# A decoder layer in fp32 on one core: normalised rows on ScalarE, the softmax factor in halves, the last products in another order, statistics at another place

## The chip, the cores and the metric

The kernel runs on one core of a Trainium2 chip. A core has engines that run side by side, each through its own list of instructions in order: TensorE (matmuls and transposes; PE in the profile, with its weight loads as PEld), VectorE (DVE), ScalarE (ACT), GpSimd (POOL), and SyncE (SP), which here issues all DMA transfers. An instruction that waits holds up everything behind it on its engine. The metric is the time of one execution on the device in microseconds (us), as the median of some runs; a profiled execution gives the trace.

## The reference

One decoder layer with three residual steps on x of shape (4, 2048, 512), fp32: a linear recurrence over the first axis (length 4), cross attention of 16 heads against 77 context rows, and a feed-forward network of hidden size 2048 whose two large matrices are followed and preceded by butterfly transforms. Each step reads a layer norm of x without gain or offset.

```python
x = x + recurrence(layernorm(x))                 # complex, diagonalised, 64 states per block of 64 features
x = x + attention(layernorm(x), ctx, Wq, Wk, Wv, Wo)   # 16 heads of 32, softmax over 77 keys
h = butterfly(layernorm(x) @ W_exp + b_exp, up_weights)
h = gelu(h + up_bias)
x = x + butterfly(h, down_weights) @ W_con + b_con + down_bias
# layernorm(x) = (x - mean) / sqrt(var + 1e-5), over the 512 features
```

## The kernel before

The 2048 columns of the second axis are cut into 16 units of 128, each with 4 rows of the first axis: a unit is a tile of 128 partitions x 4 x 512. The butterflies are multiplied into the dense matrices once, in a preparation at the start (`_prepare`, L349). The products with the dense matrices are fast-matrix-multiplication schemes: seven half-size products for queries, output projection and the up matrix (`seven`, L605; `up`, L779), and 26 products for the down matrix, in the order and with the targets of the table `DOWN` (L68). Each entry of `DOWN` names a product, a PSUM accumulator, and the parts of x that it is added to when the product is done; several products accumulate one after the other in the same accumulator, and between them its value is added to x by VectorE (L894, L896). The accumulators live in three pairs of PSUM banks, tags a, b and c (`BANK`, L73).

The work of a unit has two parts. `front` (L621) makes the three norms, the recurrence (L631), the queries (L616, ps_q), the scores (L676), the softmax (L679 to L684: minimum, exponent with sum, reciprocal of the sum, and one multiplication of all 16 heads by their factor), the transposes of the probabilities (L696) and their copies to SBUF (L699 on ScalarE, L701 on VectorE), the product with the values (L706, ps_o), the output projection (L616, ps_w) and the third norm. `feed_forward` (L753) runs eight blocks of up products with Gelu (L782 to L825), then the 26 down products (L879), then stores its rows of x (L863). While unit u is in `feed_forward`, its `step` (L765) advances `front` of unit u+1 as a generator, so that TensorE alternates between both. A tile scheduler orders each engine's list from these recordings, by its own estimates, except where `manual_schedule` (preparation, first blocks) or `keep_in_program_order` pins it.

A norm is made in three steps. `norm_stats` (L532) takes mean and variance with BN_STATS (L537) and BN_AGGR (L538) and a reciprocal root by three Newton steps on 128x4 values (L543 to L550), all on VectorE. `normed` (L553) then makes one row of 128x512 at a time with one VectorE instruction, (x - mean) * y (L563), transposes it on TensorE (L572, ps_t) and copies it with ScalarE (L573). Two row buffers (tag xn) alternate. `normed_pairs` (L576) does the same for the first norm in half rows (L590, L601, L602). After the third norm, `combine` (L742) makes the four sums of the up scheme: two on VectorE (L747, L749), two on GpSimd (L748, L750). Then the statistics of the following unit are taken (L740).

GpSimd makes the left-hand sums of the down scheme (L835), planned by `_down_plan` four products ahead. The right-hand factors of the down products lie in DRAM (dn26) and are loaded in pairs (L873) into a ring of three buffers, which the up weights of a block (L1021) share; SP issues these loads and the stores in order. The right-hand sums are made once at the hand-over from the preparation to the first unit, by GpSimd (L141) and partly VectorE (L143), and stored (L153). At the hand-over, unit 0's `front` and the preparation `prep` advance together (L981 on), where the x tile and the first statistics of unit 1 are requested at chosen steps (L984, L996).

Of the kernel before, what the change touches and what calls it, by code (L numbers as in the profile page):

```python
# [17 lines left out]
P = 128  # L18
# [52 lines left out]
        (21, "s", "+01 +11 +21"), (17, "t", "+10 +30 -01 -21"), (9, "w", "+21"), (4, "u", "+21"), (19, "z", "+10"),  # L71
        (2, "z", ""), (6, "z", "+30"), (23, "w", "+01"), (0, "u", "+31"))
# [430 lines left out]
def kernel(ctx: ExitStack, tc: tile.TileContext, x, ctx_t, ssm_vec, ssm_vt, ssm_vinv, wq_t, wk_t, wv_t,  # L503
# [49 lines left out]
    def normed(xt, res, steps):  # L553

        mv, y = norm_stats(xt)
        xnt = work.tile([P, NC, T, P], F32, tag="xnt", bufs=2, name="xnt")
        for _ in range(steps):
            yield
        rows = {}

        def row(t):
            rows[t] = work.tile([P, D], F32, tag="xn", name="xn")
            nc.vector.tensor_scalar(rows[t], xt[:, t, :], mv[:, t, 0:1], y[:, t : t + 1], ALU.subtract, ALU.mult)  # L563

        row(0)
        for t in range(T):
            if t + 1 < T:
                row(t + 1)
            yield
            ps = psum.tile([P, NC, P], F32, tag="f", name="ps_t")  # L570
            for c in range(NC):
                nc.tensor.transpose(ps[:, c, :], rows[t][:, c * P : (c + 1) * P], ident)  # L572
            nc.scalar.copy(xnt[:, :, t, :], ps)  # L573
        res.append(xnt)

    def normed_pairs(xt, res, stats):  # L576


        mv, y = stats
        xpt = work.tile([P, T // 2, D // NS, P], F32, tag="xnt", bufs=2, name="xpt")  # L580
# [4 lines left out]
        def row(n):  # L585
            i, h = divmod(n, 2)
            rows[n] = work.tile([P, NC, 2, NS], F32, tag="xn", name="xp")
            for k in range(2):
                t = 2 * i + k
                nc.vector.tensor_scalar(rows[n][:, :, k, :], xt[:, t, h * half : (h + 1) * half].rearrange("p (f n) -> p f n", n=NS),  # L590
                                        mv[:, t, 0:1], y[:, t : t + 1], ALU.subtract, ALU.mult)
# [29 lines left out]
    def front(u, xt, res, wq=None):  # L621
# [3 lines left out]
        yield from normed_pairs(xt, got, stats.pop(u) if u in stats else norm_stats(xt, tc.keep_in_program_order if u else lambda i: i))  # L625
# [11 lines left out]
        yield from normed(xt, got, 2)  # L637
# [30 lines left out]
        probs = [None] * T  # L668
        ot = work.tile([P, NC, T, P], F32, tag="xnt", bufs=2, name="ot")
        for t in range(T + 1):  # L670
            if t < T:
# [11 lines left out]
                nc.vector.reciprocal(sm, sm)  # L683
                nc.vector.tensor_tensor(pr, pr, sm.unsqueeze(2).to_broadcast([P, NH, NK]), ALU.mult)  # L684
                probs[t] = pr
                yield
            if t == 0:
                yield
                continue
            yield  # L690
            pr, tt = probs[t - 1], t - 1
            pts = work.tile([P, NC, 4, P], F32, tag="pt", bufs=1, name="pt")
            for g in range(NC):
# [4 lines left out]
                if g % 2:  # L698
                    nc.scalar.copy(pt, pt_ps[0:NK])  # L699
                else:  # L700
                    nc.vector.tensor_copy(pt, pt_ps[0:NK])  # L701
            po = psum.tile([P, NC, P], F32, tag="f", name="ps_o")
# [32 lines left out]
        yield from normed(xt, got, 4)  # L735
# [17 lines left out]
    def feed_forward(u, xt, rhs, other):  # L753
# [111 lines left out]
        for kind, where, *rest in plan:  # L865
# [31 lines left out]
            if i == 19:  # L897
                store(1)
                store(2)
            if i == 6:  # L900
                store(0, slice(0, D // 2))
                store(3, slice(0, D // 2))
            if i == 23:
                store(0, slice(D // 2, D))
# [30 lines left out]
    with ExitStack() as stack, tc.manual_schedule(engines={E.PE, E.SP, E.Pool}):  # L935
# [45 lines left out]
        for n, _ in enumerate(prep):  # L981
            if n == 27:
                _right_sums(nc, 0, wdn, rings, True)
            if n == 36:  # L984
                stats[1] = norm_stats(xts[1], tc.keep_in_program_order)
# [10 lines left out]
            if n == 24:  # L996
# [105 lines left out]
```

## Time and profile before

| | us |
|---|---|
| median of 3 runs | 2639.95 (2635.13 to 2644.54) |
| profiled execution | 2642.55 |
| its span in the trace | 2640.8 |
| one unit in the steady part (2216.1 to 2370.8) | 154.7 |
| TensorE busy in the span | 2537.6 (96%) |
| VectorE, ScalarE, GpSimd busy | 1519.4, 1071.6, 924.2 |
| mean granted TensorE clock | 0.995 of full |

In the lines of the profile a group is given by line of the kernel, engine, operation, output and inputs, with its count, its time, and the idle time before it with what ended it. In a list of waits each line has who waited for whom, the total in us, how many times, and the longest. In a timeline each line has start, duration, engine, line and operation, and in brackets the idle time just before it. A matmul in fp32 appears as two records. In the table of stretches a line has the length, the busy time and count of TensorE, its weight loads, VectorE, ScalarE and GpSimd, the granted clock, the busy share of the DMA engines and GB/s. Lines are those of the kernel before.

### The profile page before, as it was taken

How to read it: one execution, taken by the hardware profiler on the slowest of the kernel's cores; microseconds unless marked ns; L12 is line 12 of the kernel's file. 1: busy time of each engine (PE TensorE's matmuls, PEld its weight loads, DVE VectorE, ACT ScalarE, POOL GpSimd, SP SyncE). 2: the span in 40 equal slices, each digit the busy share in tenths (PEclk: the TensorE clock that was granted, in tenths of full speed). 3: DMA queues.
4: the chain of work that ended last, by engine and by line, in shares of the span. 5: the costliest groups of instructions: out<-in, count | busy, mean ns of one | idle time of the engine just before them, and what ended most of it. 6: DMA issues, size and time to landing. Idle time of an engine off the chain costs nothing.

```text
span 2640.8 us, 39542 instructions
## 1 busy us (share of the span) xinstructions
PE 2537.6 (96%) x14280; PEld 2127.7 (81%) x14280; DVE 1519.4 (58%) x3452; ACT 1071.6 (41%) x3327; POOL 924.2 (35%) x885
## 2 busy tenths in 40 slices
PE   8897999999999999999999999999999999999999
PEld 5776888787878878787887878888787878878788
DVE  6667565645646565564656556465655646465543
ACT  2452616235261523526153362624326262442621
POOL 4436422514233251422315142241514224152424
PEclk9998999999999999999999999999999999999999
DMA  5728444444545444464544446453444635344456
GB/s 177 255 80 296 162 146 161 162 154 140 209 142 168 164 153 162 136 213 136 174 144 168 154 135 215 140 181 134 164 168 136 215 132 177 144 149 168 136 185 237
DMA packets 145523, 440.70 MB, mean 167 GB/s; under 512 B 20913, under 2 KB 52785, under 8 KB 142513
## 3 DMA queue, kind: packets, MB, share of 16 engines
q1 hardware_dynamic: 145330, 438.18, 48.3%
q8 instruction: 114, 1.87, 0.3%
q14 instruction: 79, 0.65, 0.1%
HBM read 398.27 MB, written 39.86 MB: 166 GB/s over the span
## 4 chain that ended last, share of the span: by engine, by line
PE 77%; DVE 10%; ACT 8%; DMA 2%; POOL 1%; issue 1%; DVEq 0%; POOLq 0%; ACTq 0%; SPq 0%
PE ps_a L879 11%; PE ps_b L782 11%; PE ps_a L782 7%; PE ps_q L616 7%; PE ps_c L782 7%; PE ps_b L879 6%; PE ps_c L879 6%; PE ps_w L616 6%; ACT pr L681 4%; PE ps_sc L676 3%; PE ps_s L631 3%; PE ps_pt L696 3%; PE ps_o L706 2%; PE ps_t L572 2%; ACT L787 1%; ACT L681 1%
## 5 line engine op out<-in xcount | busy, mean ns | idle before, releaser
L835 POOL TENSOR_TENSOR arena<-arena 128x512 f32<-128x512 f32 x448 | 593.6, 1336 | 1457.8 <-ACT arena L787 822.3
L787 ACT ACTIVATE arena<-arena,hbias 128x256 f32<-128x256 f32 x384 | 191.7, 507 | 343.4 <-DVE arena L822 265.5
L681 ACT ACTIVATE pr<-ps_sc,low 128x77 f32<-128x77 f32 x960 | 296.6, 333 | 23.9 <-DVE low L679 22.9
L782 PE MATMUL ps_b<-arena 128*128 128x256 f32 x1128 | 293.8, 381 | 3.8 <-DVE arena L813 3.8
L573 ACT COPY xnt<-ps_t 128x512 f32<-128x512 f32 x128 | 72.0, 585 | 450.8 <-PE ps_t L572 450.8
L879 PE MATMUL ps_a<-arena 128*128 128x256 f32 x896 | 220.0, 381 | 18.8 <-DVE xt L894 12.7
L782 PEld LDWEIGHTS ps_b<-arena 128*128 128x128 f32 x1128 | 209.8, 191 | 31.3 <-DVE arena L813 4.2
L679 DVE TENSOR_REDUCE low<-ps_sc 128x4 f32<-128x308 f32 x240 | 114.7, 478 | 164.0 <-PE ps_sc L676 159.1
L681 ACT ACTIVATION_READ_ACCUMULATOR pr<-ps_sc,low 128x1 f32 x960 | 206.0, 215 | 0.0
L879 PEld LDWEIGHTS ps_a<-arena 128*128 128x128 f32 x896 | 165.5, 190 | 50.0 <-DVE xt L894 16.7
L879 PE MATMUL ps_b<-arena 128*128 128x256 f32 x768 | 201.4, 380 | 0.5 <-DVE xt L894 0.5
L782 PE MATMUL ps_a<-xnt,arena 128*128 128x256 f32 x752 | 196.3, 380 | 0.0
L676 PE MATMUL ps_sc<-kbd,qt 128*128 128x308 f32 x480 | 170.2, 442 | 0.0
L879 PE MATMUL ps_a<-w,arena 128*128 128x256 f32 x640 | 160.9, 382 | 5.9 <-ACT arena L787 5.8
L798 ACT COPY arena<-ps_a 128x256 f32<-128x256 f32 x128 | 48.2, 376 | 290.3 <-PE ps_a L782 290.3
L782 PEld LDWEIGHTS ps_a<-xnt,arena 128*128 128x128 f32 x752 | 143.3, 191 | 22.0
L696 PE MATMUL ps_pt<-ident,pr 128*77 128x128 f32 x1024 | 153.4, 279 | 4.2 <-DVE pt L701 3.9
L616 PE MATMUL ps_q<-xnt,wq 128*128 128x256 f32 x640 | 151.2, 379 | 2.2 <-POOL xnt L661 2.2
L696 PEld LDWEIGHTS ps_pt<-ident,pr 128*77 128x77 f32 x1024 | 119.2, 147 | 41.8 <-DVE pt L701 15.7
L879 PEld LDWEIGHTS ps_b<-arena 128*128 128x128 f32 x768 | 137.6, 190 | 16.0 <-DVE xt L894 0.9
L879 PEld LDWEIGHTS ps_a<-w,arena 128*128 128x128 f32 x640 | 118.8, 190 | 26.8 <-ACT arena L787 11.4
L616 PEld LDWEIGHTS ps_q<-xnt,wq 128*128 128x128 f32 x640 | 121.5, 190 | 19.0 <-POOL xnt L661 2.6
(232 smaller groups left out, 4860.9 us busy)
## 6 DMA issues: line engine op xcount, KB each, us to landing
arena<-dn SPq DMA_DIRECT2D x256, 512.0 KB, 3.9
w<-dn SPq DMA_DIRECT2D x160, 512.0 KB, 3.4
arena<-up SPq DMA_DIRECT2D x79, 896.0 KB, 4.5
wq<-wq SPq DMA_DIRECT2D x16, 1792.0 KB, 8.8
w<-up SPq DMA_DIRECT2D x32, 896.0 KB, 6.5
xt<-in_x SPq DMA_DIRECT2D x11, 1024.0 KB, 6.6
dn<-arena SPq DMA_DIRECT2D x8, 1152.0 KB, 5.8
arena<-up SPq DMA_DIRECT2D x30, 256.0 KB, 4.1
```

The lines of the kernel that those rows point to most:

```text
L572: nc.tensor.transpose(ps[:, c, :], rows[t][:, c * P : (c + 1) * P], ident)
L573: nc.scalar.copy(xnt[:, :, t, :], ps)
L616: nc.tensor.matmul(tiles[key][:, r, :], lhsT=lhs(i, r, k), rhs=rhs(i, r, k), start=key == i and r == 0 and k == 0, stop=k == 1, skip_group ...
L631: nc.tensor.matmul(ps[:, 2 * i : T, f * NS : (f + 1) * NS], lhsT=xpt[:, i, c * (P // NS) + f, :], rhs=gt[:, 0 : T - 2 * i, :], start=i == ...
L676: nc.tensor.matmul(ps[:, 0 : 4 * NK], lhsT=qt[:, g, t, :], rhs=kbd[:, t, g, :], start=True, stop=True)
L679: nc.vector.tensor_reduce(low, sc, AX.X, ALU.min)
L681: nc.scalar.activation(pr[:, 4 * g + h, :], sc[:, h, :], AF.Exp, bias=low[:, h : h + 1], scale=-1.0, accum_out=sm[:, 4 * g + h : 4 * g + h ...
L696: nc.tensor.transpose(pt_ps[0:NK, j, :], pr[:, 4 * g + j, :], ident)
L782: nc.tensor.matmul(ps, lhsT=w[:, c, :], rhs=rhs[i - 1][:, c], start=first and c == 0, stop=c == 1, skip_group_check=True)
L787: nc.scalar.activation(out, x, AF.Gelu, bias=hbias[:, b : b + 1])
L835: nc.gpsimd.tensor_tensor(place(p), place(x), place(y), ALU.add if op == "+" else ALU.subtract)
L879: nc.tensor.matmul(ps, lhsT=left[:, j, :], rhs=pair[:, n, j, :], start=first and j == 0, stop=j == NB // 4 - 1, skip_group_check=True)
```

## The change

Five things change; the arithmetic stays the same up to rounding.

- The rows of the third norm of every unit, and of all norms of unit 1, are made by ScalarE as Identity(x * y + nb) instead of VectorE. `shifts` makes nb = -mean * y with one 128x4 VectorE instruction and writes it over the means.
- The multiplication of the probabilities by their factor is split into two halves of 8 heads. For rows 1 to 3 it is recorded after the copies of the row before, and no longer before its transposes.
- The last products of `DOWN` run as 9, 19, 4, 23, 2, 6, 0 in place of 9, 4, 19, 2, 6, 23, 0.
- The stores of a unit follow product 2 (rows 1 and 2) and product 6 (row 0 whole, half of row 3), in place of products 19, 6 and 23.
- At the hand-over, the x tile of unit 1 is requested at step 15 instead of 24, and its first statistics at step 19 instead of 36.

```diff
@@ -68,8 +68,8 @@
 DOWN = ((11, "x", "+01"), (12, "y", "+30"), (5, "x", "+00"), (16, "y", "+31"), (1, "p", "+11"), (18, "q", "+20"),
         (22, "r", "+31"), (13, "o", "+00"), (25, "w", "+00"), (14, "x", "+10 +11"), (15, "y", "+21 +20"), (3, "v", "+20"),
         (20, "z", "+31"), (7, "w", "+20"), (8, "u", "-00 -10"), (10, "z", "+11"), (24, "v", "+00 +10"),
-        (21, "s", "+01 +11 +21"), (17, "t", "+10 +30 -01 -21"), (9, "w", "+21"), (4, "u", "+21"), (19, "z", "+10"),
-        (2, "z", ""), (6, "z", "+30"), (23, "w", "+01"), (0, "u", "+31"))
+        (21, "s", "+01 +11 +21"), (17, "t", "+10 +30 -01 -21"), (9, "w", "+21"), (19, "z", "+10"), (4, "u", "+21"),
+        (23, "w", "+01"), (2, "z", ""), (6, "z", "+30"), (0, "u", "+31"))
 BANK = dict(x="a", y="b", p="c", q="c", r="c", o="c", w="a", v="b", z="a", u="b", s="c", t="c")
 
 
@@ -550,9 +550,15 @@
             nc.vector.scalar_tensor_tensor(y, w, 1.5, y, ALU.add, ALU.mult)
         return mv, y
 
-    def normed(xt, res, steps):
+    def shifts(mv, y):
+
+        nc.vector.scalar_tensor_tensor(mv[:, :, 0], mv[:, :, 0], -1.0, y, ALU.mult, ALU.mult)
+        return mv[:, :, 0]
+
+    def normed(xt, res, steps, by_act):
 
         mv, y = norm_stats(xt)
+        nb = shifts(mv, y) if by_act else None
         xnt = work.tile([P, NC, T, P], F32, tag="xnt", bufs=2, name="xnt")
         for _ in range(steps):
             yield
@@ -560,6 +566,9 @@
 
         def row(t):
             rows[t] = work.tile([P, D], F32, tag="xn", name="xn")
+            if by_act:
+                nc.scalar.activation(rows[t], xt[:, t, :], AF.Identity, bias=nb[:, t : t + 1], scale=y[:, t : t + 1])
+                return
             nc.vector.tensor_scalar(rows[t], xt[:, t, :], mv[:, t, 0:1], y[:, t : t + 1], ALU.subtract, ALU.mult)
 
         row(0)
@@ -573,10 +582,11 @@
             nc.scalar.copy(xnt[:, :, t, :], ps)
         res.append(xnt)
 
-    def normed_pairs(xt, res, stats):
+    def normed_pairs(xt, res, stats, by_act):
 
 
         mv, y = stats
+        nb = shifts(mv, y) if by_act else None
         xpt = work.tile([P, T // 2, D // NS, P], F32, tag="xnt", bufs=2, name="xpt")
         half = D // 2
         yield
@@ -587,8 +597,11 @@
             rows[n] = work.tile([P, NC, 2, NS], F32, tag="xn", name="xp")
             for k in range(2):
                 t = 2 * i + k
-                nc.vector.tensor_scalar(rows[n][:, :, k, :], xt[:, t, h * half : (h + 1) * half].rearrange("p (f n) -> p f n", n=NS),
-                                        mv[:, t, 0:1], y[:, t : t + 1], ALU.subtract, ALU.mult)
+                out, x = rows[n][:, :, k, :], xt[:, t, h * half : (h + 1) * half].rearrange("p (f n) -> p f n", n=NS)
+                if by_act:
+                    nc.scalar.activation(out, x, AF.Identity, bias=nb[:, t : t + 1], scale=y[:, t : t + 1])
+                else:
+                    nc.vector.tensor_scalar(out, x, mv[:, t, 0:1], y[:, t : t + 1], ALU.subtract, ALU.mult)
 
         row(0)
         for n in range(T):
@@ -622,7 +635,7 @@
 
 
         got = []
-        yield from normed_pairs(xt, got, stats.pop(u) if u in stats else norm_stats(xt, tc.keep_in_program_order if u else lambda i: i))
+        yield from normed_pairs(xt, got, stats.pop(u) if u in stats else norm_stats(xt, tc.keep_in_program_order if u else lambda i: i), u == 1)
         xpt = got.pop()
         for c in range(NC):
             ps = psum.tile([P, T, P], F32, tag="f", name="ps_s")
@@ -634,7 +647,7 @@
             nc.vector.tensor_tensor(xc, ps, xc, ALU.add)
             yield
 
-        yield from normed(xt, got, 2)
+        yield from normed(xt, got, 2, u == 1)
         xnt = got.pop()
         qt = work.tile([P, NC, T, P], F32, tag="qt", bufs=1, name="qt")
         if wq is None:
@@ -666,6 +679,12 @@
                           4: plus(q21, q21), 3: plus(q12, q12)})
 
         probs = [None] * T
+
+        def divided(pr, sm):
+            nc.vector.reciprocal(sm, sm)
+            for h in (slice(0, NH // 2), slice(NH // 2, NH)):
+                nc.vector.tensor_tensor(pr[:, h], pr[:, h], sm[:, h].unsqueeze(2).to_broadcast([P, NH // 2, NK]), ALU.mult)
+
         ot = work.tile([P, NC, T, P], F32, tag="xnt", bufs=2, name="ot")
         for t in range(T + 1):
             if t < T:
@@ -680,15 +699,14 @@
                     for h in range(4):
                         nc.scalar.activation(pr[:, 4 * g + h, :], sc[:, h, :], AF.Exp, bias=low[:, h : h + 1], scale=-1.0,
                                              accum_out=sm[:, 4 * g + h : 4 * g + h + 1])
-                nc.vector.reciprocal(sm, sm)
-                nc.vector.tensor_tensor(pr, pr, sm.unsqueeze(2).to_broadcast([P, NH, NK]), ALU.mult)
-                probs[t] = pr
+                probs[t] = pr, sm
                 yield
             if t == 0:
+                divided(*probs[0])
                 yield
                 continue
             yield
-            pr, tt = probs[t - 1], t - 1
+            pr, tt = probs[t - 1][0], t - 1
             pts = work.tile([P, NC, 4, P], F32, tag="pt", bufs=1, name="pt")
             for g in range(NC):
                 pt_ps = psum.tile([P, 4, P], F32, tag="f", name="ps_pt")
@@ -699,6 +717,8 @@
                     nc.scalar.copy(pt, pt_ps[0:NK])
                 else:
                     nc.vector.tensor_copy(pt, pt_ps[0:NK])
+            if t < T:
+                divided(*probs[t])
             po = psum.tile([P, NC, P], F32, tag="f", name="ps_o")
             for g in range(NC):
                 for j in range(4):
@@ -732,7 +752,7 @@
         yield from seven((1, 6, 2, 7, 5, 4, 3), lambda i, r, k: left[i][:, k, r, :], lambda i, r, k: wo[:, i - 1, k, :], "w",
                          {1: spread, 6: onto(r12), 2: onto(r11), 7: onto(r22), 5: onto(r22), 4: onto(r21), 3: onto(r12)})
 
-        yield from normed(xt, got, 4)
+        yield from normed(xt, got, 4, True)
         res.append((u, xt, got.pop()))
         if u:
             combine(res[-1][2], res)
@@ -894,14 +914,12 @@
                     nc.vector.tensor_tensor(r, x, r, ALU.add)
                 else:
                     nc.vector.tensor_tensor(r, r, x, ALU.subtract)
-            if i == 19:
+            if i == 2:
                 store(1)
                 store(2)
             if i == 6:
-                store(0, slice(0, D // 2))
+                store(0)
                 store(3, slice(0, D // 2))
-            if i == 23:
-                store(0, slice(D // 2, D))
         store(3, slice(D // 2, D))
         for _ in other:
             pass
@@ -979,10 +997,10 @@
             run(prep, first)
         run(prep, prep, first, first, first, first)
         for n, _ in enumerate(prep):
+            if n == 19:
+                stats[1] = norm_stats(xts[1], tc.keep_in_program_order)
             if n == 27:
                 _right_sums(nc, 0, wdn, rings, True)
-            if n == 36:
-                stats[1] = norm_stats(xts[1], tc.keep_in_program_order)
             if n == 31:
                 _right_stores(nc, 0, wdn, rings, dn26, (2, 0))
             if n not in (24, 25):
@@ -993,7 +1011,7 @@
                 nc.gpsimd.tensor_tensor(wo[:, 6], wo[:, 2], wo[:, 6], ALU.subtract)
                 nc.gpsimd.tensor_tensor(wo[:, 5], wo[:, 2], wo[:, 4], ALU.subtract)
                 nc.gpsimd.tensor_tensor(wo[:, 3], wo[:, 1], wo[:, 5], ALU.subtract)
-            if n == 24:
+            if n == 15:
                 xts[1] = load_x(1)
             if n == 25:
                 early.append(work.tile([P, 7, 2, P], F32, tag="qt", bufs=1, name="w_second"))
```

## The prediction

> **What bounds the kernel now.** I read the busy times first, then the busy times of one steady stretch, then TensorE's waits, and then the timelines of the places where it waits.
>
> ```profile
> PE 2537.6 (96%) x14280; PEld 2127.7 (81%) x14280; DVE 1519.4 (58%) x3452; ACT 1071.6 (41%) x3327; POOL 924.2 (35%) x885
> ...
> 2216.10:2370.80 154.70, 151.00 (x850) 127.03 (x849) 89.41 (x206) 64.76 (x204) 51.05 (x44) 1.00 0.47 162
> ```
>
> TensorE is busy 2537.6 of 2640.8 us; the second line is one unit of 154.7 us with 151.0 us of TensorE at full clock. The change removes no matmul, so it can only win from the 103 us of TensorE's idle time (3.7 us in that unit). These waits make most of what I use:
>
> ```profile
> PE ps_o L706 <- DVE pt L701: 20.2, 30, 1.0
> PE ps_a L879 <- DVE xt L894: 12.7, 10, 1.3
> PE ps_t L572 <- DVE xn L563: 7.6, 5, 4.0
> ...
> PE ps_a L879 <- DVE arena L894: 6.2, 5, 1.3
> ...
> PE ps_b L782 <- DVE arena L801: 5.3, 1, 5.3
> ...
> PE ps_b L782 <- DVE arena L813: 3.8, 1, 3.8
> PE ps_c L879 <- DMA arena<-dn: 2.9, 3, 1.7
> ```
>
> Total, times and longest: the first recurs twice in each unit, the two waits on L894 are one wait once in each of 15 units (12.7 + 6.2 = 18.9 us, 1.26 each), and L563, L801 and L813 are single waits, nearly all between 195 and 250 us, where the weights' preparation hands over to the first unit.
>
> **Part 1: the last six products.** One unit's end, TensorE and then VectorE:
>
> ```profile
> 2379.31 1.89 PE L879 MATMUL ps_a<-arena 128*128 128x256 f32 x8
> 2381.03 1.46 PE L879 MATMUL ps_a<-w,arena 128*128 128x256 f32 x6
> 2383.76 3.72 PE L879 MATMUL ps_a<-arena 128*128 128x256 f32 x16 [1.27 <-DVE xt L894]
> ```
>
> ```profile
> 2380.19 1.79 DVE L747 TENSOR_TENSOR arena<-xnt 128x512 f32<-128x512 f32 x1 [0.70 <-ACT xnt L573]
> 2382.09 0.69 DVE L749 TENSOR_TENSOR arena<-xnt,arena 128x512 f32<-128x512 f32 x1
> 2382.70 0.69 DVE L537 BATCH_NORM_STATS2 st<-xt 128x6 f32<-128x512 f32 x1
> 2383.30 0.40 DVE L894 TENSOR_TENSOR xt<-ps_a,xt 128x256 f32<-128x256 f32 x1
> ```
>
> Product 19 ends near 2381.0. Its addition to x (L894) stands on VectorE behind L747, L749 and a BN_STATS, and is done at 2383.7. Product 2 accumulates into the same bank z, so it starts at 2383.76, after three matmuls of product 23 that were put ahead. In the new order 19 runs before 4, then come 23 and 2: two products of 1.73 us lie between 19 and 2. In the changed instruction order the addition of 19 also stands ahead of L747. So it is read near 2379.5 and product 2 wants the bank at 2382.8: 3.3 us of cover. Late next is the addition of 4 (bank u, behind L747, L749 and one BN_STATS, near 2383.7), which product 0 needs at 2386.2.
>
> Then TensorE enters the next unit 1.27 us earlier, while VectorE does not: L747 still starts after the last copy of L573 (2380.1). From it follow L749, the statistics of the next unit, four L590 and L801 of its first block. I put L801's end at 2391.2 where TensorE's seventh product needs it at 2391.7: 0.5 us left. I take 1.2 us for each of 15 units: 18 us, ends 0 (the wait comes back at L801) and 18.9.
>
> Its stores: SP issues five instead of six per unit, 1 MB as before. The early half store that stood ahead of the last dn loads is gone. The load of the second block's weights (896 KB) now stands behind the store of row 0, which waits for product 23's addition (near 2384.8), where before it stood behind two stores and waited for a buffer until 2387.08. That buffer now held products 23 and 2 and is free at 2384.5. Landing 5.2 us after its issue gives 2390.5; TensorE needs it near 2392.5. So it is hidden with 2 us to spare. GpSimd's sums for the new order wait at most until product 17 is done (2374.9), and the last is needed at 2386: nothing.
>
> **Part 2: the factor in halves.**
>
> ```profile
> 2473.94 1.08 PE L706 MATMUL ps_o<-pt,vsb 77*32 77x128 f32 x32 [1.01 <-DVE pt L701]
> ...
> 2471.84 1.44 DVE L684 TENSOR_TENSOR pr<-pr,sm 128x1232 f32<-128x1232 f32 x1
> 2473.20 0.68 DVE L701 COPY pt<-ps_pt 77x512 f32<-77x512 f32 x1
> ```
>
> (First line TensorE's timeline, then VectorE's.) The copy L701 that the first ps_o needs queues behind L684. With halves, about 0.7 us each, the changed order puts it between them: it ends near 2473.3, so ps_o could start 0.6 us sooner. But two instructions later TensorE needs a dn load, and that load does not move, because it is issued when a block's weights are released, before this place:
>
> ```profile
>   PEld ps_c L879: 6.7, 8
>   PE ps_c L879: 2.9, 3
> ...
> DMA to landing us min/median/max: 3.0/3.7/7.4
> ```
>
> (Who waited for the dn loads, times, and their landing.) In 8 of 15 units the weight load already waits for it; there the 0.6 us is given back at once. In the other 7 some 0.5 us stays: 3.5 us, ends 0 and 15 x 0.6 = 9. The second wait on L701 (0.38 us per unit) has ScalarE's ot copy ahead of it and stays. The second halves are needed only at the next transposes, 8 us later; 64 more instructions cost VectorE some 0.06 us each, under its 42% of idle time.
>
> **Part 3: rows on ScalarE.** Removed from VectorE: 4 rows per unit of the third norm, 738 ns each by the mean of L563, and unit 1's rows of all three norms; added: one tiny operation (0.17 us) per norm. No row of the trace is an Identity from SBUF of this shape. The nearest is Gelu with a bias, 128x256 from SBUF, 507 ns; 256 more elements cost 209 ns by the copies (585 for 128x512, 376 for 128x256): 0.72 us. [...] The order of ScalarE shows no more table loads than before.
>
> **Part 4: the hand-over, statistics sooner and unit 1's rows.**
>
> ```profile
> 202.50 2.05 PE L782 MATMUL ps_b<-arena,w_first 128*128 128x256 f32 x4 [5.29 <-DVE arena L801]
> ...
> 245.19 1.08 PE L572 MATMUL ps_t<-ident,xn 128*128 128x128 f32 x4 [3.99 <-DVE xn L563]
> ...
> 194.86 0.65 DVE L544 TENSOR_SCALAR vi<-v 128x4 int32<-128x4 int32 x1
> ```
>
> The 5.29 us go: VectorE no longer has 18 statistics instructions ahead of L801. They now stand ahead of unit 0's own third norm, 5 us of work, so its first transpose (182.34) comes 3 to 7 us later. (128x4 operations take 0.16 us when GpSimd is idle and 0.65 beside its sums, as the last line shows.) So far nothing is won. What sets the end is a chain that the change leaves: GpSimd's right-hand sums, their dn stores (6.4 us to land), then sixteen L143 on VectorE that wait for them, and behind those L813, the statistics and the rows that end at 248. With L590 (3.6 us for the first four) and L563 off VectorE, the last sums start about 1.5 us sooner and the four transposes, fed by rows of 0.72 us from ScalarE, end 1 to 3 us sooner. The x load of unit 1 is moved ahead of the first weights on SP and still waits for its tile until 159.9; the weights then land near 166, needed at 193. The w load no longer waits for L498 until 203.6, which frees 0.9 us.
>
> [...] I take 2.5 us for this part, ends -6 and +8.
>
> **Sum.** 18 + 3.5 + 0 + 2.5 = 24 us. The profiled execution took 2642.55 us (2640.8 span, 1.75 around it), so it would be 2618.5; the median of the runs shown lies 2.6 lower, at 2639.95: **2616**.
>
> **Rivals.** (A) The boundary wait returns at L801 or the xp rows because VectorE's chain from L747 isn't sooner: 0.5 us of slack speaks against it, its small size for it. Some 0.4 us kept of 1.26: 6 + 3.5 + 2.5 = 12, 2628. (B) The covers are larger than I read: 18.9 + 9 + 7 = 35, 2605; the DMA rows speak against it. (C) The reorder moves the wait to another bank, and no part does anything: 2639; the two products between speak against it. (D) Slower: at each boundary the row 0 store blocks SP ahead of the second block's weights. It decides when product 23's addition comes later than 2386.8 (2 us after my figure); each us beyond costs 15 us. To lose, it must come 3.6 us late: 2650 at 4.3 us. L747 at 1.79 us beside GpSimd is the only thing near that could stretch.
>
> **Chances.** Main case 0.63 (2609 to 2622), A 0.13, B 0.13, C 0.05, D 0.06. All but C and D are faster by over 0.3% (7.9 us, about what a measurement of this kernel can tell); a bad hand-over puts 0.01 of A within: faster 0.88, same 0.06, slower 0.06. The range leaves out C, D and half of B: 2605 to 2631.
>
> **What would show it.** Right: no wait of ps_a L879 on L894; a steady unit of about 153.2 us; waits on pt L701 near half, those on dn loads larger; the xn row on ScalarE between 0.65 and 0.85 us with no wait of ps_t in steady units; the first transpose of the hand-over later, L801's 5.3 us gone. Wrong: a new wait of ps_b L782 on L801 or of ps_a L782 on weights in every unit, or a hand-over that ends later than 250 us.

## The result and the profile after

| | before | after |
|---|---|---|
| median of 4 runs each, taken together | 2637.83 us | 2616.86 us |
| ratio, 95% interval | | 0.9919 (0.9894 to 0.9944) |
| ratio in a second set of runs | | 0.9891 (0.9871 to 0.9911) |
| span of the profiled execution | 2640.8 us | 2613.2 us |

The prediction was 2616 (2605 to 2631). The sum came out nearly right, but its terms did not: part 1 was worth more than its 18 us, part 2 about its 3.5, and part 4 nothing that these runs can tell from 0. That the sum lies so near the measured median is partly luck, as the section on the prediction says.

The page's busy times, after:

```profile
PE 2537.3 (97%) x14280; PEld 2130.7 (82%) x14280; DVE 1478.2 (57%) x3458; ACT 1126.2 (43%) x3403; POOL 923.9 (35%) x885
```

And a steady unit in the table of stretches, cut from one L769 (VectorE's second sum after the third norm) to the next:

```profile
1590.14:1742.86 152.72, 150.56 (x849) 127.05 (x849) 88.28 (x206) 67.78 (x208) 50.87 (x45) 1.00 0.48 164
```

The work moved between VectorE and ScalarE as counted (41 us less, 55 us more). The unit is 152.7 us in place of 154.7. TensorE's waits, after (total, times, longest):

```profile
PE ps_t L581 <- ACT xn L570: 13.0, 4, 5.2
PE ps_o L726 <- DVE pt L719: 11.6, 30, 0.8
...
PE ps_c L899 <- DMA arena<-dn: 5.0, 8, 1.1
PE ps_pt L714 <- DVE pt L719: 4.3, 8, 0.8
PE ps_a L802 <- ACT arena L818: 3.6, 1, 3.6
PE ps_w L629 <- DVE sw L737: 3.5, 13, 0.3
...
PE ps_b L802 <- DVE arena L833: 2.4, 1, 2.4
```

The wait on the additions (18.9 us; L894 is L914 now) is gone. The waits on the copies of the probabilities fell from 20.2 to 11.6 us, and those on dn loads rose from 2.9 to 5.0. L801's 5.3 us at the hand-over are gone, but the rows' wait grew from 7.6 to 13.0 and one wait of 3.6 us on ScalarE (L818) is new.

To tell the two regions apart I cut each profiled execution at the same two marks: the last L749 (L769) before the steady units and the last of all. Between them lie 14 units. The lines of before and after in the table of stretches:

```profile
365.21:2536.78 2171.57, 2115.90 (x11872) 1780.19 (x11871) 1251.34 (x2871) 907.06 (x2856) 715.28 (x617) 1.00 0.47 161
```

```profile
367.35:2509.75 2142.40, 2112.24 (x11868) 1780.16 (x11867) 1232.22 (x2885) 949.04 (x2912) 714.93 (x616) 1.00 0.48 163
```

14 units are 29.2 us shorter, more than the whole span lost; the first mark lies 2.1 us later.

### The profile page after: what moved, and what is told of

Same layout as the page of the kernel before. It is cut to its first block, busy times and chain, and to the rows that moved or that the text cites. A ratio compares the mean times of both kernels' runs of the same rounds, so it can differ in the third digit from the quotient of the medians.

```text
span 2613.2 us, 39583 instructions
## 1 busy us (share of the span) xinstructions
PE 2537.3 (97%) x14280; PEld 2130.7 (82%) x14280; DVE 1478.2 (57%) x3458; ACT 1126.2 (43%) x3403; POOL 923.9 (35%) x885
## 4 chain that ended last, share of the span: by engine, by line
PE 80%; ACT 8%; DVE 7%; DMA 3%; POOL 1%; issue 1%; SPq 0%; ACTq 0%; POOLq 0%
PE ps_a L899 13%; PE ps_b L802 11%; PE ps_a L802 8%; PE ps_q L629 7%; PE ps_c L802 7%; PE ps_b L899 6%; PE ps_w L629 6%; PE ps_c L899 5%; ACT pr L700 4%; PE ps_s L644 3%; PE ps_sc L695 3%; PE ps_pt L714 3%; PE ps_o L726 2%; PE ps_t L581 2%; DMA arena<-dn 2%; DVE sw L737 1%
## 5 line engine op out<-in xcount | busy, mean ns | idle before, releaser
L818 ACT COPY arena<-ps_a 128x256 f32<-128x256 f32 x128 | 48.2, 376 | 268.0 <-PE ps_a L802 268.0
L570 ACT ACTIVATE xn<-xt,mv,y 128x512 f32<-128x512 f32 x48 | 37.8, 811 | 225.6 <-DVE mv L555 225.6
```

## The experiments

Two measures are used for all runs: the time of these 14 units in the profiled execution, and the ratio of the timed runs to the kernel before.

| kernel | 14 units, us | median unit, us | ratio (95%) |
|---|---|---|---|
| before | 2171.57 | 154.71 | 1 |
| part 1 alone | 2142.88 | 153.04 | 0.9897 (0.9880 to 0.9913) |
| part 2 alone | 2165.69 | 154.54 | 0.9978 (0.9965 to 0.9991) |
| parts 1 and 2 | 2140.11 | 152.89 | 0.9890 (0.9870 to 0.9909) |
| the changed kernel | 2142.40 | 152.80 | 0.9919 (0.9894 to 0.9944) |
| the changed kernel again | 2138.70 | 152.75 | 0.9891 (0.9871 to 0.9911) |
| part 3 undone | 2141.82 | 152.98 | 0.9883 (0.9867 to 0.9899) |
| part 4 undone | 2140.18 | 152.78 | 0.9885 (0.9869 to 0.9901) |
| db in another buffer | 2138.83 | 152.86 | 0.9889 (0.9875 to 0.9902) |
| the same, statistics at step 28 | 2139.00 | 152.75 | 0.9898 (0.9883 to 0.9913) |
| two more BN_STATS per unit | 2152.84 | 153.69 | 0.9958 (0.9945 to 0.9970) |
| short loads for products 1 and 18 | 2126.87 | 151.97 | 0.9853 (0.9838 to 0.9868) |
| part 4 undone, load of product 1 split | 2133.39 | 152.30 | 0.9861 (0.9846 to 0.9876) |
| products 4 and 19 exchanged back | 2156.06 | 154.17 | 0.9950 (0.9931 to 0.9969) |

The two rows of the changed kernel show what this measure can tell: the same program differs by 3.7 us over 14 units.

### Part 1 alone

```diff
-        (9, "w", "+21"), (4, "u", "+21"), (19, "z", "+10"),
-        (2, "z", ""), (6, "z", "+30"), (23, "w", "+01"), (0, "u", "+31"))
+        (9, "w", "+21"), (19, "z", "+10"), (4, "u", "+21"),
+        (23, "w", "+01"), (2, "z", ""), (6, "z", "+30"), (0, "u", "+31"))
...
-            if i == 19:
+            if i == 2:
                 store(1)
                 store(2)
             if i == 6:
-                store(0, slice(0, D // 2))
+                store(0)
                 store(3, slice(0, D // 2))
-            if i == 23:
-                store(0, slice(D // 2, D))
```

> Only part 1: the last six products in the new order and the stores moved with them, everything else as in the kernel before. My theory: the wait of ps_a L879 on L894 (18.9 us in 15 units) goes whole, since the two products between 19 and 2 cover 3.3 us: 18 to 19 us less, a profiled execution near 2624. Rival A: without the rows moved off VectorE its chain into the next unit is too late and a wait of TensorE on L801 takes 0.4 to 0.8 us per unit back: 6 to 12 us less. Rival C: the wait moves to another bank: no change. The two halves' comparison also tells whether part 1 needs the other parts: if the parts are independent, this run and the one with the halves alone make up the whole of the 27.6 us that the profiled span lost.

Measured: 27 us less (2614.25 against 2641.37), all of what the change gives, without any of its other parts. The 14 units in the table of stretches:

```profile
364.23:2507.11 2142.88, 2109.18 (x11868) 1779.28 (x11868) 1243.87 (x2870) 906.84 (x2856) 725.89 (x615) 1.00 0.46 163
```

They are 28.7 us shorter. The waits that the list names fell by 22 us over them: 18.3 of additions, 1.9 of dn loads, 1.7 of sw. The other 6.7 us are in TensorE's busy time (2115.90 to 2109.18), though the kernel's matmuls are the same. Some 4 us of them recur (0.28 us in each unit; where they come from is said in the section on the prediction). 1.1 us is the cut: at the first mark TensorE is further ahead, so that fewer matmul records lie in the first of the 14 units. 1.6 us stand in one unit of before in which a dn load was late (152.64 us of busy time). Rivals A and C fall: the steady units show no wait on L801, and the wait did not move to another bank. Since the rows were still on VectorE, part 1 needs no help from part 3.

### Which half of part 1: products 4 and 19 exchanged back

```diff
-        (9, "w", "+21"), (19, "z", "+10"), (4, "u", "+21"),
+        (9, "w", "+21"), (4, "u", "+21"), (19, "z", "+10"),
         (23, "w", "+01"), (2, "z", ""), (6, "z", "+30"), (0, "u", "+31"))
```

> The changed kernel with products 4 and 19 exchanged again: the end runs 9, 4, 19, 23, 2, 6, 0, so that one product (23) lies between 19 and 2, and the addition of 19 stands on VectorE behind L767, L769 and one BN_STATS as in the kernel before. Everything else is as in the changed kernel. It parts the two things that part 1 does: the whole of product 23 in between is worth 0.43 us more than the three quarters of it that stood there before, the place of 19's addition the rest. Theory: 19's addition is done near 2359.5 on the changed kernel's clock and product 2 wants its bank at 2358.6: a wait of ps_a L899 on L914 of 0.8 to 0.95 us per unit, the unit at 153.6 to 154.0 us, 12 to 17 us slower than the changed kernel. Rival: one product in between is enough and 19's place is idle: no wait, 152.8 us.

Measured: the wait is back, 11.7 us in 14 units (TensorE's waits, then its timeline):

```profile
PE ps_a L899 <- DVE xt L914: 8.4, 10, 0.8
...
PE ps_a L899 <- DVE arena L914: 3.3, 4, 0.8
```

```profile
2366.97 1.99 PE L899 MATMUL ps_a<-arena 128*128 128x256 f32 x8 [0.83 <-DVE xt L914]
```

0.83 us is what the two timelines gave: 1.27 less the one quarter of product 23 (0.43 us) that now lies in between too. By the median unit, the place of 19's addition ahead of L767 is worth 1.4 us (154.17 against 152.75 to 152.80) of the 1.67 us of part 1, so it is most of it; by the sums over 14 units, with their late loads, it is 15.5 of 28.7 us. The stores stand in their new places in this run too. From before to it the median unit fell by 0.54 us, which the quarter of product 23 (0.43) and part 2 (0.15) make up, so nothing is left that the moved stores would have to explain. The price is again higher than the wait. The 14 units are 15.5 us longer than the mean of the two executions of the changed kernel (2140.55), 3.8 us more than the wait itself, and TensorE's busy time is 3.6 us higher (2114.89 against a mean of 2111.3).

### The slack at L821: two more BN_STATS

```diff
         for t in (2, 3, 0, 1):
-            keep(nc.vector.bn_stats(st[:, t, :], xt[:, t, :]))
+            for _ in range(3 if t == 2 and more else 1):
+                keep(nc.vector.bn_stats(st[:, t, :], xt[:, t, :]))
```

> The changed kernel with two more BN_STATS of 128x512 (0.65 us each) on VectorE in the statistics of the following unit, at each of 14 unit boundaries, ahead of the half rows and L821; their result is the same. It prices the cover that part 1 leans on. I put L801's end 0.5 us ahead of TensorE's need; the trace of the changed kernel shows 0.26 us (L821 ends at 2366.93, its product starts at 2367.19). Theory: 1.3 us more on VectorE shows as a wait of ps_b L802 on L821 of about 1.0 us per unit: 11 to 15 us slower than the changed kernel. Rival: VectorE has slack there that I don't see: 0 to 3 us slower.

Measured: 12.3 us over 14 units against the mean of the changed kernel's two executions, and a new wait (shown without its releaser) once per unit:

```profile
PE ps_b L803 <- issue: 9.4, 14, 1.0
```

In the timeline it lies right behind L822's end (L822 is L821 moved by a line):

```profile
2378.20 1.10 PE L803 MATMUL ps_b<-arena 128*128 128x256 f32 x4 [0.65 <-issue]
```

The wait is 0.67 us in the mean, but 1.3 us less 0.67 us is not the slack, since VectorE's order changed too: the fourth half row (L605, L604 in the changed kernel) now stands behind L822.

```profile
2377.68 0.42 DVE L822 TENSOR_TENSOR arena<-ps_b,arena 128x256 f32<-128x256 f32 x1
2378.01 0.41 DVE L605 TENSOR_SCALAR xp<-xt,mv,y 128x256 f32<-128x256 f32 x1
```

So the addition came 0.98 us later (counted from L769), not 1.3. The slack can be read in the changed kernel itself, VectorE and then TensorE:

```profile
2366.51 0.42 DVE L821 TENSOR_TENSOR arena<-ps_b,arena 128x256 f32<-128x256 f32 x1
```

```profile
2367.19 1.03 PE L802 MATMUL ps_b<-arena 128*128 128x256 f32 x4
```

L821 ends 0.26 us ahead of its product here, and 0.25 to 0.28 in the other steady units but the first (0.10). That is half of the 0.5 us of the prediction; with part 1 alone it was 1.02 us. That product, which waits, starts 0.10 us after the addition's end (2378.10 and 2378.20 above), so that in this order a VectorE chain longer by some 0.2 us at the unit's end would begin to take the gain back. The change lives that close to rival A.

### Part 2 alone, and parts 1 and 2 together

```diff
-                nc.vector.reciprocal(sm, sm)
-                nc.vector.tensor_tensor(pr, pr, sm.unsqueeze(2).to_broadcast([P, NH, NK]), ALU.mult)
-                probs[t] = pr
+                probs[t] = pr, sm
...
+            if t < T:
+                divided(*probs[t])
             po = psum.tile([P, NC, P], F32, tag="f", name="ps_o")
```

> Only part 2: the factor of the probabilities in halves, recorded after the copies, everything else as before. My prediction: 0.6 us sooner per unit, given back at once to the dn load in 8 of 15 units: 3.5 us less. What the trace of the changed kernel suggests instead: the waits on the copy fell by 8.6 us and those on dn loads grew by 2.4 us, so some 6 us stay, and the waits on sw fell by 1.9 us: 6 to 8 us less. Rival: the dn loads take all of it: 0.

> Only parts 1 and 2 (order with stores, halves); rows and statistics as in the kernel before. If parts 3 and 4 are worth nothing in the steady units and cost at the hand-over what the traces say (first query product at 257 to 259 without them, 259.4 with them), this kernel is 0 to 3 us faster than the changed one, with the same steady unit of 152.8 us. If the changed kernel needs parts 3 and 4 for its gain, it is slower than it by 3 us or more.

Measured: part 2 alone takes 5.9 us off the 14 units and 0.22% (0.09 to 0.35%) off the time; on top of part 1 it takes 2.8 us. The median unit says 0.17 and 0.15 us, which is about 2.5 us over 15 units. So 2.5 to 6 us, about the predicted 3.5. The place in the changed kernel (TensorE's timeline):

```profile
2447.55 1.19 PE L726 MATMUL ps_o<-pt,vsb 77*32 77x128 f32 x32 [0.37 <-DVE pt L719]
2448.67 0.79 PE L695 MATMUL ps_sc<-kbd,qt 128*128 128x308 f32 x2
2449.61 0.70 PE L899 MATMUL ps_c<-arena 128*128 128x256 f32 x2 [0.15 <-DMA arena<-dn]
```

The wait of 1.01 us is 0.37 us, the predicted 0.6 us less, and two lines on TensorE waits for the dn load. With parts 1 and 2 alone the unit is the changed kernel's, and so is the time (2609.5 and 2610.63 in the same set of runs).

### Part 3 undone

```diff
-        yield from normed(xt, got, 4, True)
+        yield from normed(xt, got, 4, False)
```

(and the same for unit 1's other norms)

> The changed kernel with part 3 undone: all rows again on VectorE, shift and scale as subtraction and multiplication there; order, halves and the place of the statistics stay. My theory: 0 in the steady units (the rows lie under other work on either engine), within 1 us per 15 units. At the hand-over ScalarE's rows stood, in the changed kernel, behind a buffer that is released by a GpSimd addition at 203.7, and cost TensorE 3.6 us there; with the rows on VectorE that wait goes or turns into one on VectorE's rows: minus 4 to plus 4 us. Rival: the rows on ScalarE are what makes the reorder pay, since they empty VectorE: then 4 x 0.65 us of rows come back ahead of the unit's end and this kernel is 5 to 15 us slower than the changed one.

Measured: 2141.82 us for the 14 units, between the two executions of the changed kernel (2138.70 and 2142.40), and a ratio of 0.9883 against 0.9919 and 0.9891. Where the rows are made is worth nothing that these runs can tell; the rival, that the reorder needs them off VectorE, falls.

### Part 4 undone

```diff
-            if n == 19:
+            if n == 36:
                 stats[1] = norm_stats(xts[1], tc.keep_in_program_order)
...
-            if n == 15:
+            if n == 24:
                 xts[1] = load_x(1)
```

> The changed kernel with part 4 undone: x tile of unit 1 requested at step 24 and its first statistics at step 36 again; rows, halves and order stay. My prediction put part 4 and the rows of unit 1 together at 2.5 us less. The traces now say 0: the first transpose waits 5.2 us in place of 0.8, L801's 5.3 us are gone, ScalarE's L818 brings 3.6, and the first query product starts at 259.37 in place of 259.17. Expected here: the first transpose near 182.3 again, a stall of about 5 us before the second product of block 0, the first query product between 257 and 262: minus 2 to plus 3 us against the changed kernel.

The first query product of unit 1 starts at 255.73, sooner than the 257 to 262 that I expected. The hand-over, from TensorE's last ten matmul records of the preparation ahead of unit 0's third norm (a mark whose place in TensorE's order no part moves) to unit 1's first query product:

| kernels | us |
|---|---|
| before; part 1; part 2; parts 1 and 2 (all with the old hand-over) | 82.0; 80.8; 83.3; 81.8 |
| the changed kernel, two executions | 83.4; 79.3 |
| the same hand-over in three other runs (more BN_STATS; short loads; 4 and 19 exchanged) | 83.4; 84.1; 79.0 |
| part 3 undone | 81.4 |
| part 4 undone; with the split load | 79.9; 81.2 |
| db in another buffer; the same with the statistics at step 28 | 81.6; 79.7 |

The kernels of the first row share their hand-over and differ by 2.5 us; the changed kernel differs from itself by 4.1, and the five executions of its hand-over by 5.0. No placement leaves this band. Stalls did change: part 4 undone starts the first transpose at 181.55 and has 4.45 us before L821, as expected, against these two in the changed kernel:

```profile
185.62 1.11 PE L581 MATMUL ps_t<-ident,xn 128*128 128x128 f32 x4 [5.17 <-ACT xn L570]
...
205.63 2.08 PE L802 MATMUL ps_a<-xnt,w_first 128*128 128x256 f32 x4 [3.60 <-ACT arena L818]
```

### The new stall at L818: db in another buffer, and the statistics between

ScalarE's timeline of the changed kernel shows where the second one comes from:

```profile
198.62 0.59 ACT L494 COPY arena<-ps_p 128x512 f32<-128x512 f32 x1 [0.27 <-PE ps_p L490]
203.75 0.60 ACT L602 ACTIVATE xp<-xt,mv,y 128x256 f32<-128x256 f32 x1 [4.54 <-POOL ybias L1027]
204.26 0.56 ACT L494 COPY arena<-ps_p 128x512 f32<-128x512 f32 x1
204.72 0.60 ACT L602 ACTIVATE xp<-xt,mv,y 128x256 f32<-128x256 f32 x1
205.23 0.35 ACT L818 COPY arena<-ps_a 128x256 f32<-128x256 f32 x1
```

The second half row of unit 1 takes an xn buffer that held db, the down bias, until GpSimd had added it (L1027). It waits 4.54 us, and L818, for which TensorE waits, stands behind it.

```diff
-        db = work.tile([P, D], F32, tag="xn", name="db")
+        db = work.tile([P, NH * NK], F32, tag="pr", name="db")[:, 0:D]
```

> The changed kernel with one buffer moved: the row db (down bias) no longer takes one of the two xn buffers but one of the free pr buffers. In the changed kernel the second half row of unit 1 on ScalarE waits until 203.7 for GpSimd's addition that reads db, and the copies L494 and L818 stand behind it on ScalarE; TensorE waits 3.6 us and then runs at half rate for about 6 us. My theory: that stall goes, L818 is done near 200.4, and the hand-over ends 3 to 6 us sooner (first query product near 254 to 256). Rival: the chain of GpSimd's sums, their stores and L143 limits the end as it did before the change, and the gain is handed to a wait further on: 0 to 1 us.

```diff
-            if n == 19:
+            if n == 28:
                 stats[1] = norm_stats(xts[1], tc.keep_in_program_order)
```

(on top of the one above)

> As the kernel with db apart, and unit 1's first statistics made at step 28 in place of 19, so that they stand behind unit 0's third norm on VectorE, but ahead of its sums for block 0. My theory: the 5.2 us ahead of the first transpose go back to 0.8 and L821 still isn't late, so TensorE enters block 0 some 4 us sooner; then the chain of the sums and stores sets the end. Against the kernel with db apart: 0 to 4 us less, the first query product between 251 and 256. If the sums' chain is the bound, nothing is won and the idle time appears between 215 and 245.

Measured: with db apart the 3.6 us stall is gone, and the hand-over takes 81.6 us, inside the band. (The first query product starts at 261.75 and not near 255, but the first mark lies 4.2 us later in this profile too.) The wait before the late up product, 2.4 us in the changed kernel, is now

```profile
PE ps_b L802 <- DVE arena L833: 4.7, 1, 4.7
```

and the chain of work through the hand-over runs over GpSimd's sums and their stores:

```profile
206.97 8.23 DMA dn<-arena
...
219.63 7.44 DMA dn<-arena
227.10 0.43 DVE arena L143
...
231.12 3.22 DVE arena L143 x4
```

In both executions of the changed kernel that chain ran another way: over the addition of db, L494, L818 and TensorE's matmuls to L647, which stands ahead of the last L143. So the stall did lie on the chain, but the stores' chain was close behind: L143 end 57.5 and 54.6 us after the first mark in the two executions with the stall, and 54.2 with db apart. Against the faster of the two, 0.4 us was won, as the rival of that run said. In the other run the 5.17 us in front of the first transpose became 1.23, but 2.90 and 1.70 us appeared at 197 and 200, and 3.51 before L833: the hand-over takes 79.7 us, again inside the band. Neither of the two gains that I expected can be told from the scatter.

### The cap on part 2: shorter and split dn loads

```diff
-            nc.sync.dma_start(out=pair[:, n], in_=dn26[SLOT[str(i)]])
+            js = slice(0, 1) if i in (1, 18) else slice(0, NB // 4)
+            nc.sync.dma_start(out=pair[:, n, js], in_=dn26[SLOT[str(i)]][:, js])
```

> The changed kernel with three quarters of the dn loads of products 1 and 18 left out (128 KB in place of 512 KB; the rest of the buffer keeps old values, so those two products are wrong). It prices the cap on part 2: if the dn load for product 1 is what takes part of the halves' gain back, the waits of ps_c on dn (5.0 us, 8 times) vanish: 4 to 6 us less. Rival: the wait just moves to what stands next in the queue, the loads of products 22 and 13 or the second wait on L719: 0 to 1 us less.

Measured: 14 us less over 14 units than the changed kernel, 0.8 us per unit, more than expected, and no waits on dn are left. But this run does not prove the cap: the scheduler, which plans with shorter loads, also moved some of TensorE's instructions, among them the first matmul of product 1 (two records in the trace) to a place ahead of ps_o, where it fills part of the copy's wait. Therefore a second run, in which TensorE's instructions stand exactly as in the run with part 4 undone:

```diff
-            nc.sync.dma_start(out=pair[:, n], in_=dn26[SLOT[str(i)]])
+            for js in (slice(0, 2), slice(2, 4)) if i == 1 else (slice(0, 4),): nc.sync.dma_start(out=pair[:, n, js], in_=dn26[SLOT[str(i)]][:, js])
```

> The changed kernel with the statistics of unit 1 late again (as in the run that undid part 4), and the dn load of product 1 issued as two loads of 256 KB in place of one of 512 KB; the order of TensorE's instructions is the same as in that run, unlike in the run with shortened loads, where the scheduler also put two matmuls of product 1 ahead of ps_o. It prices the cap on part 2 alone: if the late dn load is what gives the halves' gain back, half of it lands earlier, the waits of ps_c on dn fall from 3.7 us to under 1.5, the unit goes from 152.8 to between 152.0 and 152.5 and loses its scatter: 4 to 10 us less than with part 4 undone, near 2604. Rival: the 0.8 us per unit of the shortened loads came from the two matmuls in front of ps_o: then 0 to 2 us less.

Measured: the first half seldom comes late. In the 14 units it lands 3.8 us after its issue in the median (3.1 to 5.2), where the whole load took 4.9 with part 4 undone (4.6 to 5.8). The edit did a second thing: the scheduler put the other half some 14 us ahead of the first (issued at 1504.76 and 1518.95 in one unit), so that nothing waits for it. How much each of the two gave is not separated. Weight loads that waited for dn, with part 4 undone:

```profile
PEld ps_c L899 <- DMA arena<-dn: 10.3, 14, 1.5
```

and with the load split:

```profile
PEld ps_c L899 <- DMA arena<-dn: 1.5, 3, 0.9
```

The unit is 152.30 us in place of 152.78 (6.8 us over 14 units), and 2603.23 us stand against 2610.63 for the changed kernel in the same set of runs. The cap is real and worth 0.48 us per unit. This kernel computes everything, and has the lowest ratio here of those that do: 0.9861 (0.9846 to 0.9876).

### The changed kernel again

> The changed kernel once more, unaltered, beside the next two on the same chip, so that its distance to them can be read from one set of runs. Expected: ratio to the kernel before between 0.989 and 0.994, first query product at 259.4 or a little around it, a steady unit of 152.8 us.

Measured as expected but for the hand-over: the first query product starts at 255.29, not 259.37. It serves as the comparison for the two runs beside it, and shows the scatter of the profiles.

## Why the prediction was right, and where it was not

**Part 1, 18 us: right in mechanism, too small.** The cover of 3.3 us is there. In the changed kernel (TensorE's timeline, then VectorE's) product 19's addition ends at 2355.29, and product 2, the second half of the x16 line, starts at 2358.56:

```profile
2355.10 1.89 PE L899 MATMUL ps_b<-arena 128*128 128x256 f32 x8
2356.83 3.62 PE L899 MATMUL ps_a<-arena 128*128 128x256 f32 x16
```

```profile
2354.87 0.42 DVE L914 TENSOR_TENSOR xt<-ps_a,xt 128x256 f32<-128x256 f32 x1 [1.74 <-PE ps_a L899]
```

The runs put the part at 25 us by the median unit (1.67 us x 15) and 28.7 us over 14 units by the sums. The mis-sized term is "1.2 us for each of 15 units": it took the idle time in front of one instruction, 1.26 us, for the whole price of the stall. The lines show the rest. Without a stall the next matmul starts 0.16 us ahead of the end of the one before (the x8 line lasts 1.89 us, and its follower starts 1.73 us after it); idle time is counted only from that end, so behind a stall these 0.16 us are lost as well and show as busy. And the x16 line behind the stall took 3.72 us, 0.10 more than here. 1.26 + 0.16 + 0.10 is 1.52 us; with 0.12 us less of sw wait this is 1.64 of the 1.67 us. The run with 4 and 19 exchanged shows the same: 0.83 us of idle time, and 1.1 us per unit by the sums. In three units of the profile of before a dn load was late as well, which the sums contain. My upper end of 18.9 us excluded what happened. Why the first matmul behind a stall takes 0.10 us longer, the runs do not show.

**The slack at L801, 0.5 us:** 0.26 us in the changed kernel, 1.02 with part 1 alone. Rival A stayed away, by half of the margin that I took.

**Rival D** needed the row 0 store to hold up the second block's weights. They are issued 2.8 us ahead of the unit's first up product in the changed kernel (2360.96 and 2363.74), 2.9 in the prediction's working, and no steady unit waits for them.

**Part 2, 3.5 us:** 2.5 to 6 us. The copy comes 0.6 us sooner and the dn load takes much of it back, as said; the split load recovered 0.48 us per unit. In the units where the weight load did not wait before the change, less stays than the 0.5 us that I took: there the dn load landed only 0.15 to 0.33 us ahead of it, which fits the 0.15 to 0.17 us of the median unit. The added instructions cost VectorE more than the 0.06 us each that I took: with part 2 alone its busy time in the 14 units was 1267.52 us in place of 1251.34, 16.2 us for 56 more instructions or 0.29 us each.

**Part 3, 0 us:** right, with a wrong duration on the way. No run of the kernel before shows this term; what the runs showed in its place: with part 3 undone the 14 units take 2141.82 us, between the two executions of the changed kernel (2138.70 and 2142.40). The row takes 815 ns, not 720:

```profile
L570 ACT ACTIVATE xn<-xt,mv,y x48: 797/815/822, 184.8 to 2505.1; 128x512 f32<-128x512 f32 x48
```

The Gelu row that I scaled has its scale as a constant, where the Identity has scale and bias both per partition; why the row takes 95 ns more than my estimate, no run shows. The difference moved nothing, since the four rows have 1.5 us and more to spare in the steady units: the fourth ends at 2353.14 in the unit shown under part 1, and its transpose starts at 2354.67.

**Part 4, 2.5 us: not confirmed, and not refuted.** The first transposes came 3.3 us later than before, within the 3 to 7 foretold, and L801's wait went. The step "the last sums start about 1.5 us sooner and the four transposes ... end 1 to 3 us sooner" came out both ways. In the first execution of the changed kernel VectorE's L143 end at 233.49 in place of 233.53, and the transposes at 250.6 in place of 249.94; in the second they end at 230.57 and 246.3. From the first mark of the hand-over to the end of the transposes it is 72.8 us before, and 74.6 and 70.3 after. The prediction did not have the wait of ScalarE's row behind db, which cost TensorE 3.6 us, nor that one more tiny operation (L555) would take 1.19 us, at 243.55 with GpSimd busy from 242.24 to 247.17, where its median is 0.16. No run shows the 2.5 us: the mean of the five executions of the new hand-over is 81.8 us, that of the four of the old one 82.0.

The sum came near by terms that miss in opposite directions: part 1 with 7 to 11 us too little, part 4 with 2.5 us for which no run speaks. And the first set of runs lay on the high side: the same program gave 2616.86 us (ratio 0.9919) there and 2610.63 (0.9891) in the second. So the gain itself is due to the mechanism of part 1; the nearness to 2616 is luck.

## What to carry to other kernels

An accumulator that is reused needs the reader of its old value early in that reader's own queue: exchanging two products, which put one 0.4 us addition ahead of 2.5 us of VectorE work, was worth more than everything else in this change. Count a recurring stall of TensorE at more than the idle time shown in front of one instruction (here 0.26 us more). When a faster step only brings the next wait forward (here a dn load), fix that wait in the same edit, as the split load did; and where executions of one program differ by 4 us in a phase, do not look for a gain of 2.5 us there in single profiles.

## What the runs showed of the hardware

The same gap was followed by slow matmuls in one execution and not in the other. In the two executions of the changed kernel TensorE waited 3.60 and 3.58 us for L818; the first lines behind it:

```profile
205.63 2.08 PE L802 MATMUL ps_a<-xnt,w_first 128*128 128x256 f32 x4 [3.60 <-ACT arena L818]
207.50 1.91 PE L802 MATMUL ps_b<-arena,w_first 128*128 128x256 f32 x4
```

```profile
205.37 1.13 PE L802 MATMUL ps_a<-xnt,w_first 128*128 128x256 f32 x4 [3.58 <-ACT arena L818]
206.34 1.03 PE L802 MATMUL ps_b<-arena,w_first 128*128 128x256 f32 x4
```

The granted clock between 200 and 210 us was 0.71 and 1.00. Three more runs have the same hand-over, with gaps of 3.58 to 3.59 us at this place. All five:

| | changed kernel | again | more BN_STATS | short loads | 4 and 19 exchanged |
|---|---|---|---|---|---|
| first line behind the gap (x4), us | 2.08 | 1.13 | 2.07 | 2.07 | 1.13 |
| TensorE idle in the hand-over, us | 16.4 | 16.4 | 16.5 | 16.4 | 16.4 |
| TensorE busy in the hand-over, us | 67.0 | 62.9 | 66.9 | 67.7 | 62.6 |
| granted clock in the hand-over | 0.86 | 0.91 | 0.86 | 0.84 | 0.91 |

The idle time is the same in all five, so the whole difference of 4 to 5 us between the two kinds lies in TensorE's busy time, at a lower granted clock. Why the same gap was followed by slow matmuls in three executions and not in two, no run shows. A later gap of 2.4 to 2.5 us, before L833's product, was followed by x4 lines of up to 1.91 us in the same three executions and of 1.03 in the other two. This scatter is why I could not settle part 4 to better than some 4 us.
